# Depthwise convolutions of one layer in units of 32 channels of all batches, with the neighbouring units' preparation and finishing beside each

## Chip, cores and metric

The kernel runs on one core of a Trainium2 chip. The metric is the device time of one execution in microseconds (us); the median of several executions is given. A profile is one such execution with every engine's instructions recorded: TensorE (PE for matmuls, PEld for loading its weights), VectorE (DVE), ScalarE (ACT), GpSimd (POOL), SyncE (SP), and the DMA queues.

## The reference

Four layers, each adding a function of its group-normalised input to x of shape (4, 384, 64, 64), float32. The change is in the third, "layer 2":

```python
def layer2(x, ...):          # x: group-normalised, 4 x 384 x 64 x 64
    ...                      # gate (B), kw (B x 2, softmax): two small nets on the channel means of x
    y3 = _bn(_dw(x, c3_w, 1), c3_g, c3_b)      # depthwise 3x3
    y5 = _bn(_dw(x, c5_w, 2), c5_g, c5_b)      # depthwise 5x5
    y1 = x * c1_w + c1_b
    tok = _bn(kw[:, 0:1] * y3 + kw[:, 1:2] * y5 + y1, ar_g, ar_b)
    gp = tok.mean(axis=(2, 3), keepdims=True)
    gh = _gelu(_bn(_pw(gp, cg_w1), cg_g1, cg_b1))
    gates = sigmoid(_bn(_pw(gh, cg_w2), cg_g2, cg_b2))
    tok = tok * gates
    h1 = _gelu(_bn(_pw(tok, cm_w1), cm_g1, cm_b1))   # 384 -> 768 channels
    h2 = _bn(_pw(h1, cm_w2), cm_g2, cm_b2)           # 768 -> 384
    return gate * (tok + h2) + (1.0 - gate) * x

def _bn(x, g, b):            # statistics over batch, height and width, per channel
    m = x.mean(axis=(0, 2, 3)); v = x.var(axis=(0, 2, 3))
    return (x - m) * rsqrt(v + EPS) * g + b
```

So a channel's y3 and y5 can be normalised only when the convolution of that channel is finished in all four batches, and the gates need the mean of tok over every channel.

## The kernel before

The channels are 3 chunks (j) of 128; P = 128, N = 4096 (one image), B = 4, C = 384. Layer 2's convolutions are done on PE as products with banded matrices: the strips `z` hold, for one channel, two image rows (128 values) as partitions and (row pair, batch) as columns; `toep` is a matrix made from the channel's weights and a band of ones. One step makes both convolutions of two channels:

```python
def conv53(self, j, c0, st):                 # 64 times in a chunk
    if c0 % 8 == 0:
        self.w53 = ...                       # weights of 8 channels, DMA by SP
        self.d_o = self.bt_p.tile([P, 2, 8, P], F32, tag="d_o", name="d_o")
    t = self.bt_p.tile([P, 24, 8, 8], F32, tag="toep", name="toep53", bufs=3)
    eng, band = (nc.gpsimd, self.band7) if c0 // 2 % 5 in (1, 3) else (nc.vector, self.band7_p)
    eng.tensor_tensor(t, <w53, broadcast>, <band, broadcast>, ALU.mult)         # L1026
    m = self.psum.tile([P, 512], F32, tag="c", name="conv_m", bufs=3)
    for c in range(2):
        for i in range(3):
            nc.tensor.matmul(m[:, c * 256 : (c + 1) * 256], lhsT=self.z_[...], rhs=t[...], ...)   # L1036
    nc.scalar.copy(self.d_o[:, :, at : at + 2], mv)                              # L1045
    for c in range(2):
        for v in range(2):
            nc.vector.bn_stats(st[:, v, c0 + c], self.d_o[:, v, at + c])         # L1048
    if at == 6:
        for v in range(2):                   # 128-value runs to DRAM, on ACT's queue
            nc.scalar.dma_start(self.d53[v][j][c0 - 6 : c0 + 2].rearrange("c y b n -> (y b) c n"), self.d_o[:, v])
```

`strips5` brings x1 (the layer's input) from DRAM into strips, 1024 or 2048 values of 128 channels of one batch at a time; `to_strips5(j, b)` does so for one batch:

```python
def strips5(self, j, b, x, k0, psum):
    nc.sync.dma_start(x, self.x1[b][:, j, k0 * P : (k0 + n) * P])
    nc.scalar.activation(x, x, AF.Identity, bias=self.n2[:, j, b : b + 1], scale=self.r2[:, j, b : b + 1])
    for i in range(n // 4):
        m = psum("strip_m")
        for k in range(4):
            nc.tensor.transpose(m[:, k * P : (k + 1) * P], x[:, at : at + P], self.ident)   # L1008
        zv = self.z[:, :, 1 + k0 + 4 * i : 5 + k0 + 4 * i, b]
        if i % 2: nc.vector.tensor_copy(zv, mv)      # L1012
        else:     nc.scalar.copy(zv, mv)             # L1014
```

`conv_norms(j, st)` makes the batch norms' statistics of a chunk (two matmuls for the mean over partitions, `cn_rep`; eight into `cn_m`; a chain of small DVE operations; a root by ACT as exp and ln, L301 and L302). `toks(j)` finishes a chunk: 16 blocks, each reading x1 and the two convolutions' results from DRAM:

```python
def toks(self, j):                           # a generator; each yield ends one block
    for b in range(B):
        for q in range(4):
            src = {k: self.bc_p.tile([P, 1024], F32, tag=k, name=f"c_{k}") for k in ("x1", "d5", "d3")}
            ...                              # three DMAs by SP, L1114 and L1116
            tok = src["x1"] if j < NJ - 1 else self.tok_last[:, b, sl]
            for i in range(2):
                nc.scalar.activation(m, src["x1"][:, part], AF.Identity, bias=at(self.s0), scale=at(self.s1))     # L1123
                nc.vector.scalar_tensor_tensor(m, src["d3"][:, part], at(self.s3), m, ALU.mult, ALU.add)          # L1124
                nc.vector.scalar_tensor_tensor(tok[:, part], src["d5"][:, part], at(self.s5), m, ..., accum_out=total[...])   # L1126
            nc.scalar.activation(src["d3"], tok, AF.Square, bias=at(self.about), accum_out=squares[...])          # L1135
            if j < NJ - 1:
                nc.sync.dma_start(self.scratch["tok"][b][j][:, sl], tok)
            ...
```

`tok_last` lies in the memory of the strips, which are no longer needed then. The order of all this:

```python
def phase_b(self):
    self.to_strips5(0, B - 1)                # chunk 0's other batches were made during layer 1
    self.nets(cp)                            # the two small nets
    for j in range(NJ):
        st = ...
        toks = self.toks(j - 1)
        for c0 in range(0, P, 2):
            self.conv53(j, c0, st)
            if c0 % 10 == 8:
                next(toks, None)
        self.conv_norms(j, st)
        if j + 1 < NJ:
            for b in range(B):
                self.to_strips5(j + 1, b)
                next(toks, None)
        ...
    for _ in self.toks(NJ - 1):
        pass
```

Then `phase_ef`: the gates (a chain of small matmuls, L1196 to L1207), and the two projections. For each batch and block of 1024, the first projection:

```python
t01 = io.tile([P, NJ - 1, 1024], F32, tag="tok", name="e_tok")        # two buffers
t = [t01[:, 0], t01[:, 1], self.tok_last[:, b, blk]]
for j in range(NJ):
    if j < NJ - 1:
        nc.sync.dma_start(t[j], self.scratch["tok"][b][j][:, blk])
    nc.vector.tensor_scalar(t[j], t[j], self.at[...], self.ct[...], ALU.mult, ALU.add)   # L1235
...
for o in range(6):
    ...                                       # six matmuls 128x512 into h_s, L1250
```

## Time and profile before

Three executions: 5185.74, 5191.8 and 5192.47 us; median 5191.8. The profiled one has a span of 5184.7 us.

| engine | busy us | share | instructions |
|---|---|---|---|
| PE, matmuls | 4661.8 | 90% | 17899 |
| PEld, weight loads | 2572.5 | 50% | 17899 |
| DVE | 2773.1 | 53% | 4900 |
| ACT | 2054.1 | 40% | 2656 |
| POOL | 672.5 | 13% | 506 |

The granted clock of PE was 0.942 of full speed on average; DMA moved 723.23 MB, 139 GB/s over the span. Layer 2's convolutions begin at 2621.6 us of the span and end at 3231; the first projection's matmuls begin at 3341. In a row of groups the columns are: line, engine, operation, output and inputs, shapes, count; busy us in total and mean ns of one; then the idle time of the engine just ahead of these instructions and what ended it ("<-"). PE's records overlap in the pipeline, so the pace of a stretch of them, and not one record's length, tells what one costs.

### The profile page before, as it was taken

The page shows a single profiled execution, that of the slowest core. Times are in us where ns is not written, and L with a number is a line of the kernel's source. Part 1 is how long each engine was busy: PE and PEld are TensorE (multiplying, and loading weights), DVE is VectorE, ACT ScalarE, POOL GpSimd, SP SyncE. Part 2 cuts the span into 40 slices and gives each one's busy share as a digit, 9 for nine tenths or more (in the row PEclk, how much of TensorE's full clock was granted, in tenths as well). Part 3 has the DMA queues.
Part 4 walks back from the last instruction along what each step waited for, and adds up shares of the span by engine and source line. Part 5 has one row for each costly group of instructions (what it writes and reads, how often), then busy time and mean ns, then how long its engine had stood idle before and what let it go on. Part 6 is the DMA issues. An engine that isn't in the chain of part 4 may idle for free. (4 is left out here: it accounts for less than half of the span.)

```text
span 5184.7 us, 47837 instructions
## 1 busy us (share of the span) xinstructions
PE 4661.8 (90%) x17899; PEld 2572.5 (50%) x17899; DVE 2773.1 (53%) x4900; ACT 2054.1 (40%) x2656; POOL 672.5 (13%) x506
## 2 busy tenths in 40 slices
PE   5999999999999999999898989299999995649999
PEld 2333444334343443445377878144444442548999
DVE  5322456634565355556766988654421114658775
ACT  4544344454454444433134453511223334552320
POOL 1000000000000000000043434000000000125433
PEclk9999999999999999989988999599999997559999
DMA  5210211111111111123156989866644434557776
GB/s 163 67 48 28 88 61 61 55 62 37 60 63 66 42 43 55 61 75 100 57 169 179 348 249 284 281 227 238 246 170 166 149 134 174 215 178 247 223 222 191
DMA packets 470822, 723.23 MB, mean 139 GB/s; under 512 B 18251, under 2 KB 315958, under 8 KB 464438
## 3 DMA queue, kind: packets, MB, share of 16 engines
q1 hardware_dynamic: 330792, 519.45, 31.4%
q10 hardware_dynamic: 114510, 105.99, 6.0%
q0 software_dynamic: 25280, 94.65, 4.7%
q8 instruction: 144, 2.36, 0.2%
q14 instruction: 96, 0.79, 0.0%
HBM read 440.82 MB, written 279.18 MB: 139 GB/s over the span
## 5 line engine op out<-in xcount | busy, mean ns | idle before, releaser
L724 PE MATMUL av<-probs,vt 128*97 128x512 f32 x2048 | 955.4, 601 | 0.0
L693 ACT ACTIVATE probs<-sc_s 128x1024 f32<-128x1024 f32 x512 | 499.5, 1021 | 756.6 <-PE av L724 739.3
L724 PEld LDWEIGHTS av<-probs,vt 128*97 128x97 f32 x2048 | 319.3, 165 | 503.3 <-issue 499.7
L1036 PE MATMUL conv_m<-toep,z 128*128 128x256 f32 x2304 | 506.5, 382 | 13.0 <-ACT d_o L1045 7.6
L909 DVE SCALAR_TENSOR_TENSOR acc<-band,vecs,acc 128x512 f32<-128x512 f32 x696 | 493.5, 747 | 42.7 <-POOL band L870 25.0
L1299 PE MATMUL h_m<-f_h,cm_w_t 128*128 128x512 f32 x1152 | 496.4, 594 | 7.9 <-ACT f_h L1289 7.9
L1036 PEld LDWEIGHTS conv_m<-toep,z 128*128 128x128 f32 x2304 | 439.7, 192 | 78.5 <-issue 10.4
L1250 PE MATMUL h_s<-e_tok,cm_w_t 128*128 128x512 f32 x768 | 363.7, 596 | 5.1 <-DVE e_tok L1235 5.1
L1583 PE MATMUL conv_m<-toep,z 128*128 128x128 f32 x3072 | 363.8, 277 | 1.0 <-DVE rest_o L1591 1.0
L1299 PEld LDWEIGHTS h_m<-f_h,cm_w_t 128*128 128x128 f32 x1152 | 219.4, 191 | 284.9 <-issue 273.1
L1583 PEld LDWEIGHTS conv_m<-toep,z 128*128 128x128 f32 x3072 | 354.8, 193 | 1.5 <-issue 1.2
L1026 POOL TENSOR_TENSOR toep<-w,band 128x1536 f32<-128x1536 f32 x78 | 268.3, 3439 | 360.5 <-PE conv_m L1036 280.8
L685 PE MATMUL sc_s<-q,k 32*128 32x512 f32 x2048 | 299.6, 643 | 16.3 <-ACT probs L693 11.6
L832 PE MATMUL t_m<-w_in_t,xb 128*128 128x384 f32 x768 | 282.5, 501 | 7.9 <-DVE coef L849 3.6
L757 PE MATMUL proj_m<-xm,w_proj_t 128*128 128x512 f32 x576 | 265.2, 599 | 0.8 <-DVE xm L710 0.8
L1257 ACT COPY e_h<-h_s 128x1024 f32<-128x1024 f32 x96 | 97.2, 1012 | 398.9 <-PE h_s L1250 398.9
L764 DVE SCALAR_TENSOR_TENSOR x_res<-proj_m,bn_c,x_res 128x512 f32<-128x512 f32 x96 | 71.8, 748 | 334.2 <-PE proj_m L757 334.1
L1250 PEld LDWEIGHTS h_s<-e_tok,cm_w_t 128*128 128x128 f32 x768 | 146.9, 191 | 190.0 <-issue 184.4
L1307 DVE BATCH_NORM_STATS2 h_st<-f_h 128x6 f32<-128x512 f32 x72 | 50.0, 694 | 322.9 <-ACT f_h L1306 322.9
L1026 DVE TENSOR_TENSOR toep<-w,band_p 128x1536 f32<-128x1536 f32 x114 | 199.2, 1748 | 36.2 <-PE conv_m L1036 29.0
L832 PEld LDWEIGHTS t_m<-w_in_t,xb 128*128 128x128 f32 x768 | 141.6, 192 | 150.6 <-issue 65.5
L1045 ACT COPY d_o<-conv_m 128x512 f32<-128x512 f32 x192 | 111.1, 583 | 259.5 <-PE conv_m L1036 225.7
(360 smaller groups left out, 6328.9 us busy)
## 6 DMA issues: line engine op xcount, KB each, us to landing
d<-d_o ACTq DMA_DIRECT2D x96, 512.0 KB
c_d<-d SPq DMA_DIRECT2D x96, 512.0 KB
hid<-e_h ACTq DMA_DIRECT2D x16, 3072.0 KB
f_h<-hid SPq DMA_DIRECT2D x16, 3072.0 KB
x_res<-in_x SPq DMA_DIRECT2D x32, 768.0 KB
x_in<-in_x SPq DMA_DIRECT2D x96, 256.0 KB
xa<-x_res POOLq DMA_DIRECT2D x32, 768.0 KB, 3.9
xa_in<-xa SPq DMA_DIRECT2D x32, 768.0 KB
```

Source lines behind the costliest of these rows:

```text
L685: nc.tensor.matmul(s[:, g], lhsT=k4[32 * g : 32 * g + 32, c], rhs=q[i][32 * g : 32 * g + 32], start=True, stop=True,)
L693: nc.scalar.activation(p[:, h * 1024 : (h + 1) * 1024], s[:, 2 * h : 2 * h + 2].rearrange("p a b -> p (a b)"), AF.Exp, scale=0.25,)
L724: nc.tensor.matmul(av[0 : PD + 1, :], lhsT=vt[:, 4 * c + v, :], rhs=p[:, v * 512 : (v + 1) * 512], start=c == 0 and v == 0, stop=c == 7 an ...
L757: nc.tensor.matmul(m, lhsT=self.w_proj[:, j, o * P : (o + 1) * P], rhs=xm[:, j], start=j == 0, stop=j == NJ - 1,)
L832: nc.tensor.matmul(m[:, 0:C], lhsT=xb[:, j], rhs=self.w_in[:, j, :], start=j == 0, stop=j == NJ - 1,)
L909: nc.vector.scalar_tensor_tensor(out, src(j, k), w, done, ALU.mult, ALU.add)
L1026: eng.tensor_tensor(t, self.w53[:, at : at + 192].rearrange("p (m n) -> p m n", n=8).unsqueeze(2).to_broadcast([P, 24, 8, 8]), band.rearra ...
L1036: nc.tensor.matmul(m[:, c * 256 : (c + 1) * 256], lhsT=self.z_[:, at : at + P], rhs=t[:, 12 * c + 4 * i : 12 * c + 4 * i + 4].rearrange("p ...
L1045: nc.scalar.copy(self.d_o[:, :, at : at + 2], mv)
L1250: nc.tensor.matmul(s[:, v, :], lhsT=w1[:, j, o * P : (o + 1) * P], rhs=t[j][:, v * 512 : (v + 1) * 512], start=j == 0, stop=j == NJ - 1,)
L1299: nc.tensor.matmul(m, lhsT=w2[:, o, j * P : (j + 1) * P], rhs=h[:, o, v * 512 : (v + 1) * 512], start=o == 0, stop=o == 5,)
L1583: nc.tensor.matmul(m[:, ch * P : (ch + 1) * P], lhsT=self.z_[:, at : at + P], rhs=t[:, 8 * c + 2 * i : 8 * c + 2 * i + 2].rearrange("p m a ...
```

## The change

The convolutions are no longer done in three chunks of 128 channels with standing borders, but in 12 units of 32 channels, each of all four batches at once, so that a tile's 128 partitions are 4 batches × 32 channels. While unit u is convolved, the strips of unit u + 1 are made (odd steps) and unit u − 1 is finished (even steps). Further:

- the banded matrices are made two steps ahead, by DVE and POOL in turn (before 3 to 2);
- the statistics of two channels are taken by one instruction: it keeps those of its even and odd elements apart, and so gets the two channels' elements in turn (2 of 256 elements a step instead of 4 of 128);
- a unit's normalised x stays in SBUF for its tok; x1 is not read a second time, but chunk 0's x1 is read again, as its strips were made in another layout;
- the results of the convolutions lie in DRAM so that writes are runs of 1024 values and reads runs of 128;
- tok of every unit goes to DRAM, the last chunk's too;
- `swap` changes statistics between "a channel per partition" and "batch × 32 channels per partition", with one matmul, at the start and at the end of the stage.

```diff
 def phase_b(self):
-    self.to_strips5(0, B - 1)
+    self.taps53(0)
+    for n in range(2):
+        self.matrices53(n)
+    for q in range(4):
+        x = self.bx_p.tile([P, 2048], F32, tag="x", name="in_x1")[:, 0:1024]
+        self.strips5(0, B - 1, x, 8 * q, self.pm)
+    self.units(cp)                       # norms of x1 in the units' layout (swap)
     self.nets(cp)
-    for j in range(NJ):
-        ...
+    for _ in self.unit_strips(0):
+        pass
+    for u in range(UNITS):
+        st = self.bt_p.tile([P, 2, 16, 6], F32, tag="st", name="st")
+        strips = self.unit_strips(u + 1) if u + 1 < UNITS else iter(())
+        tok = self.unit_tok(u - 1) if u else iter(())
+        for n in range(16):
+            self.matrices53(16 * u + n + 2)
+            self.conv53(u, n, st)
+            next(strips if n % 2 else tok, None)
+        self.conv_norms(u, st)
+    for _ in self.unit_tok(UNITS - 1):
+        pass
+    self.tok_stats()                     # means and variances of tok, back by swap
...
+def unit_strips(self, u):
+    j, q = u // 4, u % 4
+    for i in range(2):
+        x = self.bx_p.tile([P, 2048], F32, tag="x", name="unit_x")      # five buffers
+        for b in range(B):
+            nc.sync.dma_start(x[32 * b : 32 * b + 32], self.x1[b][32 * q : 32 * q + 32, j, i * 2048 : (i + 1) * 2048])
+        self.unit_x[u].append(x)
+        for h in range(4):
+            if h % 2 == 0:
+                nc.scalar.activation(xh, xh, AF.Identity, bias=..., scale=...)
+            if j:
+                m = self.pm("strip_m")
+                for k in range(4):
+                    nc.tensor.transpose(m[:, k * P : (k + 1) * P], x[:, at : at + P], self.ident)
+                if h == 3:
+                    nc.vector.tensor_copy(zv.rearrange("p c k b -> p k b c"), mv)
+                else:
+                    nc.scalar.copy(zv, mv.rearrange("p k b c -> p c k b"))
+            yield
...
 # in conv53
-    for c in range(2):
-        for v in range(2):
-            nc.vector.bn_stats(st[:, v, c0 + c], self.d_o[:, v, at + c])
+    for v in range(2):
+        nc.vector.bn_stats(st[:, v, n], self.d_o[:, v, at : at + 2].rearrange("p c n -> p n c"))
...
-                self.d53[v][j][c0 - 6 : c0 + 2].rearrange("c y b n -> (y b) c n"), self.d_o[:, v]
+                self.d53[v][u][:, :, 2 * n - 6 : 2 * n + 2].rearrange("y b c n -> (y b) (c n)"),
+                self.d_o[:, v].rearrange("p c n -> p (c n)"),
...
+def unit_tok(self, u):                   # as toks, but x from self.unit_x[u], four blocks, and always:
+        nc.sync.dma_start(self.tok[u, :, :, sl].rearrange("b c n -> (b c) n"), d5)
...
 # in phase_ef
-    t = [t01[:, 0], t01[:, 1], self.tok_last[:, b, blk]]
+    at = i % 3 * 1024                    # i: the block of the batch, 0 to 3
+    t = [t01[:, 0], t01[:, 1], self.z_[:, at : at + 1024]]
     for j in range(NJ):
-        if j < NJ - 1:
-            nc.sync.dma_start(t[j], self.scratch["tok"][b][j][:, blk])
+        for q in range(4):
+            nc.sync.dma_start(t[j][32 * q : 32 * q + 32], self.tok[4 * j + q, b, :, blk])
```

`conv_norms` keeps its form, with one `cn_rep` matmul of 64 columns and four one-column matmuls into `cn_m`, once per unit.

## The prediction

> **What bounds the kernel now.** I read the page's time slices first, then windows cut at the events of layer 2, then the groups, waits and pieces of the timeline there. TensorE is busy 90% of the span, so a change here can win only where PE stands or does other work than convolving and projecting. The windows of layer 2's convolutions and what follows (columns: length; busy us and instructions of PE, weight load, DVE, ACT, POOL; granted clock; DMA share; GB/s):
>
> ```profile
> 2621.60:2792.00 170.40, 169.75 (x774) 147.93 (x774) 121.67 (x310) 52.38 (x83) 88.98 (x26) 0.99 0.50 142
> 2792.00:2840.00 48.00, 32.42 (x149) 24.80 (x149) 28.38 (x52) 31.90 (x35) 0.33 (x1) 0.68 0.77 225
> 2840.00:3019.00 179.00, 170.44 (x768) 146.94 (x768) 160.07 (x400) 79.70 (x125) 89.28 (x26) 0.98 0.93 304
> 3019.00:3059.00 40.00, 26.40 (x139) 19.04 (x139) 24.33 (x45) 28.64 (x31) 0.18 (x1) 0.83 0.86 251
> 3059.00:3231.00 172.00, 168.51 (x780) 146.32 (x778) 160.03 (x405) 74.45 (x124) 86.06 (x25) 1.00 0.92 292
> ```
> ```profile
> 3231.00:3325.00 94.00, 5.45 (x20) 4.42 (x20) 54.30 (x144) 46.53 (x72) 0.00 (x0) 0.52 1.10 326
> 3325.00:3341.00 16.00, 1.90 (x12) 1.73 (x12) 9.20 (x38) 13.78 (x20) 0.00 (x0) 0.50 0.28 110
> 3341.00:3840.00 499.00, 497.14 (x1151) 219.80 (x1152) 252.11 (x386) 99.73 (x101) 11.50 (x16) 0.99 0.60 225
> ```
>
> Lines 1, 3 and 5 are the three chunks of convolutions, PE all but full. Lines 2 and 4 are the borders: statistics, then the strips of the next chunk (transposes and copies), with no convolution. The first line of the second fence is the tail: the last chunk's tok, PE empty, DMA over its full share. Then the small chain of gates, then the projections, PE full again. In 2621.6–3341 PE convolves in five sixths of the time; the rest is what the change aims at. The waits of 3231–3345 say what each engine of the tail stands for:
>
> ```profile
> PE cg_z L1201 <- DVE gp L1196: 90.2, 1, 90.2
> DVE tok_m L1124 <- DMA c_d<-d: 20.4, 12, 3.1
> ```
>
> PE has one wait of 90.2 us, for channel means that need all of tok; inside it DVE waits for tiles from DRAM. A block of tok (1024 of a batch) starts every 4.9 us there. The price list of the operations concerned, from the groups of 2540–3300:
>
> ```profile
> L1026 POOL TENSOR_TENSOR toep<-w,band 128x1536 f32<-128x1536 f32 x78 | 268.3, 3439 | 360.5 <-PE conv_m L1036 280.8 <-DVE toep L1026 35.1 <-DMA w<-in_c_t 19.4
> L1026 DVE TENSOR_TENSOR toep<-w,band_p 128x1536 f32<-128x1536 f32 x114 | 199.2, 1748 | 36.2 <-PE conv_m L1036 29.0 <-issue 6.9
> L1048 DVE BATCH_NORM_STATS2 st<-d_o 128x6 f32<-128x128 f32 x768 | 165.5, 280 | 35.1 <-ACT d_o L1045 35.0
> L1045 ACT COPY d_o<-conv_m 128x512 f32<-128x512 f32 x192 | 111.1, 583 | 259.5 <-PE conv_m L1036 225.7 <-DMA d<-d_o 30.5 <-issue 2.1
> L1014 ACT COPY z<-strip_m 128x512 f32<-128x512 f32 x36 | 38.4, 1072 | 28.4 <-PE strip_m L1008 28.4
> L1012 DVE COPY z<-strip_m 128x512 f32<-128x512 f32 x36 | 38.7, 1074 | 29.2 <-PE strip_m L1008 29.1
> ```
>
> The borders are seen to the microsecond in the timeline: convolution resumes at these points (start, length; in brackets the wait ahead):
>
> ```profile
> 2839.97 23.55 PE L1036 MATMUL conv_m<-toep,z 128*128 128x256 f32 x108 [1.26 <-DVE z L1012]
> ...
> 3341.03 6.55 PE L1250 MATMUL h_s<-e_tok,cm_w_t 128*128 128x512 f32 x8 [5.08 <-DVE e_tok L1235]
> ```
>
> [...] 0.52 in the tail against 0.99 to 1.00 beside it, so every long stand costs a little more after it. [...] the trace shows 1.28 us. Twelve statistics chains instead of three bring more loads. [...] chunk 1, mostly 512-byte pieces, moves 142 GB/s at a share of 0.50 (284 per full share), the projections, in larger pieces, 225 at 0.60 (375). So the 4-KB writes of the new layout should help. [...] DVE's toep reads its band from PSUM, and of POOL's idle time only 35.1 us are put down to DVE's toep. I count POOL at its 3.44 us.
>
> **The change part by part.**
>
> *Convolutions themselves.* In the undisturbed 2700–2750 PE does 233 records in 50.00 us, 0.2146 each; a step of two channels has 12, so 2.575 us; 192 steps are 494.4 us. This stays. Before, 2621.6–3231 is 609.4: 494.4, borders of 48.6 (2791.4 to 2839.97) and 44.1 (3018.3 to 3062.46), and 22.3 lost inside the chunks.
>
> *Borders.* What goes is their standing. The transposes do not: chunks 1 and 2 need 64 groups of four at 0.66 us (one such group in the timeline), 42.2 us of PE between convolutions. So of 92.7 us at most 50.5 come free.
>
> *New on PE's path.* Statistics run 12 times, each with a rep matmul, four small ones, and some waiting for DVE between: I estimate 1.8 us of PE each, 22, mostly because PE's queue runs in order and holds the next convolution back. The last transposes of a unit stand right ahead of the next unit's first convolution in PE's order, whose copy by ACT or DVE (1.07) and semaphores cost an estimated 2 us at the eight such borders: 16. Inside losses 10 to 15 instead of 22.3, since the stats and writes are lighter but tok and strips run beside every step. The first steps of the stage: 4.
> Sum: 494.4 + 42.2 + 22 + 16 + 4 + 12 = 590.6, against 609.4: −19.
>
> *Other engines, per unit of 16 steps (about 49 us).* DVE: 8 toep × 1.75 = 14.0; statistics 32 of 256 elements, from 0.22 at 128 and 0.64 at 512 in runs, about 0.36 each, 11.5 (before 64 × 0.22 = 14); two strip copies 2.1; tok 8 × (0.75 + 0.74 + 0.08) = 12.6; the chain 3.3. Together 43.5, 89%. ACT: d_o 16 × 0.58 = 9.3, normalise and tok about 4.2 + 6.2, Squares 5.4, six strip copies at 0.64 to 1.07, table loads and DMA issues: some 39. POOL: 8 × 3.44 = 27.5. None exceeds PE, but DVE runs in order with little room. DMA: 2.1 MB of x, 1.6 of taps, 4.2 written, 4.2 read, 2.1 of tok: 14.2 MB in 49 us, 290 GB/s; chunk 2 ran at 304. It fits, with no reserve.
>
> *Start.* The first strips come in quarters with copies behind them, against whole halves: −4, an estimate; the new layout exchange (one small matmul) eats little of it.
>
> *Tail.* From the last convolution (3231) to the first projection (3341.03) are 110 us, 94 of them for a whole chunk's tok. Now one unit, a twelfth, is left: statistics 11 (before, first tok at 3247.6, but with larger statistics and weight loads ahead of it), writing and reading the last convolutions (inside that and a few us more), four blocks at an estimated 3.2 (4.9 × 2 of 3 tiles read), 27 to here; final sums and layout exchange 4; the gates' chain 16, plus some 3 as its weights' DMAs are issued by ACT only behind the last Square. Together 50: −60.
>
> *Projections.* All tok comes from DRAM now, four DMAs of 32 partitions per chunk. Chunk 2's third uses three places in the strips' buffer, by block number modulo 3; block 3 of a batch and block 0 of the next share place 0, so that load waits for the last matmul of the block. The block's last group leaves PE 4 matmuls × 0.854 = 3.4 us of other work; load, scale and start I put at 8 (estimate from the 4.9 us cadence with DVE behind it). +4.5 at three borders: +13.
>
> Sum: −4 −19 −60 +13 = −70; 5191.8 − 70 = 5122.
>
> **The rivals.** (a) *The convolution stage gains nothing or grows.* In its favour: chunk 2's DVE was at 160.07 of 179 us with the load now spread over all units; DVE waits in order for tok's reads, and a late read holds up toep, hence PE; twelve statistics chains with ACT's table loads. Against: the matrices are two steps ahead and the stats are cheaper. It would turn the −19 into 0 to +40: 5141 to 5181. (b) *All of it hides.* If transposes fill PE's gaps without stops, statistics cost 1 us, and the projections never wait, the floor is 494.4 + 42.2 + 12 + 10 = 559, tail 45, no projection loss: −50 −65 −4 = −119, about 5073. Against: two dozen handovers between engines in each unit. (c) *The projections turn DMA-bound.* They read 8.4 MB more than before in the same 499 us, 17 GB/s over 225 at a share of 0.60: as a rate no danger; only the shared place speaks for it. If each of 16 blocks waited 3 us, +48: 5160.
>
> **Range and chances.** The tail is the sure part (−50 to −65). The convolution stage runs from −45 to +20 about −19, the projections 0 to +30. Together 5085 to 5168 in eight of ten. Two per cent is 5088: faster 0.13, within 0.84, slower (over 5295.6) 0.03.
>
> **What would show it.** Right: first convolution to last about 590 us, PE's clock near 1.0 with no window of it under 0.9; the gap from the last convolution to the first h_s about 50, clock at half in it; in the projections three waits of h_s for DVE's scaling of the strips' buffer, about 4.5 each; toep 96 on each engine, statistics 384 of 256. Wrong: statistics nearer 0.55 each than 0.36 (reading every second channel may be slow), which would put 6 us more on DVE per unit and make it the bound; POOL's toep well above 3.44; long conv_m waits for toep; or the tail at 70 because of late weights.

## The result and the profile after

Four executions of the changed kernel: median 5163.4 us (5156.27 to 5167.02), against 5192.1 for the kernel before (four executions, 5185.74 to 5192.96). The ratio is 0.9946, with a 95% interval of 0.9928 to 0.9963. The kernel is faster by 28.7 us, half a per cent; the prediction was 5122, a gain of 70.

The two profiled executions, cut at the same events of PE (first and last convolution of layer 2, first product of the first projection, first of the second):

| stretch | before, us | after, us | change | predicted |
|---|---|---|---|---|
| start of the span to layer 1's last norm | 2599.6 | 2607.4 | +7.8 | 0 |
| from there to the first convolution | 22.0 | 21.0 | −1.0 | −4 |
| convolutions, first to last | 609.3 | 627.7 | **+18.4** | **−19** |
| tail: last convolution to first h_s | 110.1 | 54.8 | −55.2 | −60 |
| projections: first h_s to first h_m | 507.5 | 524.4 | +16.9 | +13 |
| the rest | 1336.2 | 1330.0 | −6.2 | 0 |

The first and last rows are work that the change does not touch; over all runs of this study the first lies between 2599 and 2613. So totals below are compared by medians of several executions, and stretches by profiles. The tail and the projections came out within 5 us of what was predicted. The convolutions (from here on "the stage") were to give 19 us and took 18 more.

Windows of the changed kernel (columns as in the prediction's windows; units 0 to 3, units 4 to 10, unit 11, the tail, the projections):

```profile
2628.40:2849.00 220.60, 191.20 (x843) 163.58 (x839) 164.56 (x316) 109.45 (x164) 110.03 (x32) 0.93 0.75 225
2849.00:3210.10 361.10, 330.78 (x1638) 286.00 (x1638) 295.18 (x603) 207.75 (x322) 192.83 (x56) 1.00 0.92 275
3210.10:3256.20 46.10, 44.53 (x200) 38.40 (x200) 38.48 (x85) 22.87 (x37) 20.67 (x6) 0.96 0.88 274
3256.20:3311.00 54.80, 4.16 (x25) 3.52 (x25) 23.80 (x95) 28.34 (x41) 0.00 (x0) 0.55 0.89 258
3311.00:3827.50 516.50, 503.83 (x1152) 221.81 (x1152) 258.35 (x391) 99.67 (x101) 11.47 (x16) 0.98 0.63 233
```

No engine is full in the first line: of 220.6 us DVE works 164.56, ACT 109.45, POOL 110.03. PE's 191.20 contains time at a granted clock of 0.50 (30.7 of the 220.6 us; 0.93 on average). Units 4 to 10 take 361.10 / 7 = 51.6 us each, every one alike; the prediction's 590.6 is 49.2 on average. Units 0 to 3 take 55.3, 53.7, 50.7 and 60.9, although units 0 to 2 have no transposes beside them, as chunk 0's strips were made during layer 1. Of the names below, `d_o` is ACT's copy of a convolution's result out of PSUM, `unit_x` a unit's x, `st` a unit's statistics, `cn_...` and `about` the values of the chain that `conv_norms` makes of them ("the chain"), `c_d` and `tok_m` tok in the making.

What PE waited for between the first and last convolution (columns: us in total, times, longest):

```profile
PE conv_m L1122 <- ACT d_o L1131: 17.6, 9, 5.6
PE strip_m L1051 <- ACT unit_x L1044: 11.7, 8, 1.8
PE cn_rep L1149 <- DVE st L1134: 7.2, 9, 1.5
PE conv_m L1122 <- DVE toep L1103: 5.5, 3, 3.2
PE conv_m L1122 <- DVE about L1189: 5.4, 1, 5.4
```

PE waits for ACT to empty a PSUM buffer, once in each of nine units (first line), and eight times for x that ACT has yet to normalise (second). The last line bears the name of the last DVE operation that ended before PE went on, but no convolution reads `about`. The timeline of unit 3 (columns: start, length, engine, instruction; in brackets the wait ahead) shows what PE waited for:

```profile
2802.65 3.41 POOL L1103 TENSOR_TENSOR toep<-w,band 128x1536 f32<-128x1536 f32 x1 [1.75 <-PE conv_m L1122]
2802.86 3.22 DVE L1186 TENSOR_TENSOR about<-c_u,cn_s 128x1 f32<-128x1 f32 x1
...
2806.00 1.74 DVE L1103 TENSOR_TENSOR toep<-w,band_p 128x1536 f32<-128x1536 f32 x1
...
2807.89 1.19 PE L1122 MATMUL conv_m<-toep,z 128*128 128x256 f32 x2 [5.39 <-DVE about L1189]
```

DVE's matrix for this step ended at 2807.74, 0.15 us ahead of PE, and stood behind an addition of one column that took 3.22 us. Another 1.3 us, at the start of unit 3, are put down to `cn_d` in the same way. So matrices (toep), which the prediction watched, cost PE 5.5 + 5.4 + 1.3 = 12.2 us, all of them DVE's; no wait of PE is put down to one of POOL's. The groups of the same operations in the changed kernel:

```profile
L1103 POOL TENSOR_TENSOR toep<-w,band 128x1536 f32<-128x1536 f32 x96 | 330.4, 3442 | 313.3 <-PE conv_m L1122 254.3 <-issue 35.3 <-DMA w<-in_c_t 14.5
L1103 DVE TENSOR_TENSOR toep<-w,band_p 128x1536 f32<-128x1536 f32 x96 | 166.1, 1745 | 11.0 <-PE conv_m L1122 10.8
L1134 DVE BATCH_NORM_STATS2 st<-d_o 128x6 f32<-128x256 f32 x384 | 149.7, 423 | 87.4 <-ACT d_o L1131 87.0
L1189 DVE TENSOR_TENSOR about<-about,cn_mean 128x1 f32<-128x1 f32 x24 | 28.4, 1183 | 0.1
```

POOL's and DVE's matrices have the durations that were taken for them (3442 and 1745 ns). The statistics take 423 ns each; by the prediction's measure, busy time over count, they take 0.39 us (149.7 / 384), not 0.36. The last line is the odd one: 24 additions of one column take 1183 ns on average. Seen one by one (columns: shortest, median, longest ns, first and last start) they are mostly short:

```profile
L1189 DVE TENSOR_TENSOR about<-about,cn_mean x24: 136/160/3354, 2704.1 to 3263.5; 128x1 f32<-128x1 f32 x24
```

Ten of over 2 us make up 26 of the 28.4.

Unit 5, one of the seven alike, shows what happens:

```profile
2912.25 3.45 POOL L1103 TENSOR_TENSOR toep<-w,band 128x1536 f32<-128x1536 f32 x1 [2.21 <-PE conv_m L1122]
...
2913.14 2.58 DVE L1189 TENSOR_TENSOR about<-about,cn_mean 128x1 f32<-128x1 f32 x1
...
2915.64 0.74 DVE L1212 SCALAR_TENSOR_TENSOR tok_m<-c_d,cn_s,tok_m 128x512 f32<-128x512 f32 x1
2916.30 0.15 DVE L1189 TENSOR_TENSOR about<-about,cn_mean 128x1 f32<-128x1 f32 x1
...
2918.76 0.73 DVE L1214 SCALAR_TENSOR_TENSOR c_d<-c_d,cn_s,tok_m 128x512 f32<-128x512 f32 x1
...
2919.53 1.15 ACT L1219 ACTIVATE c_d<-c_d,about 128x1024 f32<-128x1024 f32 x1 [5.64 <-DVE c_d L1214]
...
2920.68 0.56 ACT L1131 COPY d_o<-conv_m 128x512 f32<-128x512 f32 x1
...
2921.38 1.53 PE L1122 MATMUL conv_m<-toep,z 128*128 128x256 f32 x6 [1.51 <-ACT d_o L1131]
```

POOL's matrix runs from 2912.25 to 2915.70. DVE's addition starts inside it and ends at 2915.72. Its twin, a moment later and outside POOL's matrix, takes 0.15. The 2.4 us go down the chain: DVE's tok is late, ACT's Square (L1219) stands 5.64 for it, the next d_o copy is behind the Square in ACT's order and starts at 2920.68, though its convolutions ended at 2914.70, and PE, whose three PSUM buffers are full, stands 1.51. It was not the matrix that came late: that of this step, POOL's of 2912.25, had been ready for 5.7 us. Then PE stands 1.4 more for a transpose, as ACT comes late to normalise x as well. In unit 1 the same chain made PE stand 5.6 and then work for 3.0 us at a granted clock of 0.50 (2712.49 to 2715.52).

The whole stage shows the same: of DVE's additions, products and differences with both inputs in SBUF that began while at least 0.5 us of one of POOL's matrices was left (2400 to 3300 us), 16 of 16 lasted to that matrix's end. Of tok's operations of 128x512 with one input in PSUM, 77 did so and none was held (at most 0.775 us). What in the chip makes it so, no run shows.

The tail and the projections of the changed kernel, PE's longest waits:

```profile
PE swap_m L1021 <- DVE swap L1019: 26.1, 1, 26.1
PE cg_z L1292 <- DMA cg_w_t<-in_cg_w_t: 13.4, 1, 13.4
```
```profile
PE h_s L1342 <- DVE z L1327: 12.6, 4, 4.0
PE h_s L1342 <- DVE e_tok L1327: 5.1, 1, 5.1
```

PE first stands 26.1 us for the last unit's tok, then 13.4 for the gates' weights. In the projections it stands four times, 12.6 us together, for chunk 2's scaling in the strips' buffer: 1.6 in the first block (1.8 before), and 3.9, 4.0 and 3.2 at the three borders between batches. The 5.1 is the start, 5.08 before.

### The profile page after: what moved, and what is told of

Its sections match the earlier page's. It is cut to its first block, busy times and chain, and to the rows that moved or that the text cites. A ratio compares the mean times of both kernels' runs of the same rounds, so it can differ in the third digit from the quotient of the medians.

```text
span 5165.3 us, 48069 instructions
## 1 busy us (share of the span) xinstructions
PE 4669.4 (90%) x17963; PEld 2579.1 (50%) x17963; DVE 2742.2 (53%) x4606; ACT 2093.9 (41%) x2736; POOL 734.3 (14%) x524
## 5 line engine op out<-in xcount | busy, mean ns | idle before, releaser
L1122 PE MATMUL conv_m<-toep,z 128*128 128x256 f32 x2304 | 527.4, 389 | 33.5 <-ACT d_o L1131 17.6
L1103 POOL TENSOR_TENSOR toep<-w,band 128x1536 f32<-128x1536 f32 x96 | 330.4, 3442 | 313.3 <-PE conv_m L1122 254.3
L1351 DVE BATCH_NORM_STATS2 h_st<-e_h 128x6 f32<-128x512 f32 x192 | 123.4, 685 | 203.7 <-ACT e_h L1349 203.7
L1342 PE MATMUL h_s<-z,cm_w_t 128*128 128x512 f32 x384 | 198.3, 600 | 12.6 <-DVE z L1327 12.6
```

The source lines that it names most:

```text
L1103: eng.tensor_tensor(t, self.w53[:, at : at + 192].rearrange("p (m n) -> p m n", n=8).unsqueeze(2).to_broadcast([P, 24, 8, 8]), band.rearra ...
L1342: nc.tensor.matmul(s[:, v, :], lhsT=w1[:, j, o * P : (o + 1) * P], rhs=t[j][:, v * 512 : (v + 1) * 512], start=j == 0, stop=j == NJ - 1,)
L1351: nc.vector.bn_stats(st[:, o, 8 * b + 2 * i + v, :], h[:, o, v * 512 : (v + 1) * 512])
```

## The experiments

Theory A: the small operations of the statistics chain are held by POOL's matrices, and that delay goes through ACT's order to PE. Theory B: the chain, with ACT's table loads and twelve handovers, is long by itself, or ACT and DVE are simply too full; the long additions are only where the waiting shows. Further questions were what the chain costs in all, the place shared in the projections, late weights at the start and in the tail, and what the two other parts of the change (two channels in one instruction, longer runs) are worth. All ratios are to the kernel before on the same chip; its medians there lay between 5187.9 and 5194.2 us, so medians of different runs are compared to within some 6 us only.

| run | median us | ratio, 95% interval | convolutions, us |
|---|---|---|---|
| after | 5163.4 | 0.9946 (0.9928 to 0.9963) | 627.7 |
| e1: chain with one input in PSUM | 5183.4 | 0.9977 (0.9967 to 0.9987) | 645.5 |
| e2: no chain in units 1 to 11 | 5117.3 | 0.9855 (0.9832 to 0.9878) | 586.8 |
| e3: own place per block | 5148.5 | 0.9919 (0.9896 to 0.9941) | 625.4 |
| e4: taps earlier | 5160.1 | 0.9938 (0.9915 to 0.9961) | 623.8 |
| e5: no matrices by POOL | 5107.5 | 0.9842 (0.9816 to 0.9867) | 568.4 |
| e6: short chain | 5120.2 | 0.9856 (0.9827 to 0.9886) | 581.6 |
| e7: short chain, Sqrt | 5124.8 | 0.9877 (0.9851 to 0.9904) | 575.1 |
| e8: gates' weights early | 5166.1 | 0.9949 (0.9929 to 0.9968) | 625.0 |
| e9: together | 5102.7 | 0.9811 (0.9787 to 0.9835) | 576.4 |
| e10: e6, four statistics a step | 5128.9 | 0.9880 (0.9863 to 0.9897) | 596.9 |
| e11: matrices 3 to 2 | 5144.1 | 0.9899 (0.9881 to 0.9917) | 607.0 |
| e12: e6, runs of 512 bytes | 5125.2 | 0.9866 (0.9851 to 0.9882) | 588.5 |

### e1: the chain with one input in PSUM

```diff
-        mean = self.sm([P, 2], "cn_mean")
+        mean = own(64, 2)          # own: 80 columns of the PSUM bank that holds DVE's band
-            nc.vector.tensor_mul(a[:, v : v + 1], a[:, v : v + 1], ...)
+            nc.vector.tensor_mul(a_s[:, v : v + 1], a[:, v : v + 1], ...)     # a in PSUM, a_s in SBUF
...                                 # and so on: of two inputs always one in PSUM
```

> In the changed kernel the twelve statistics chains hold DVE operations of one or two columns that last up to 3.35 us instead of 0.15, always until a banded matrix on POOL ends. Here each such operation reads one of its two inputs from PSUM, and the copy of the means into four blocks is an addition of a zero from PSUM; the values are the same. Theory A (DVE is locked out by POOL while it reads two SBUF inputs, ACT stands behind the chain with the copies that free the convolution's PSUM, and so PE stands): no operation of the chain over 0.7 us, the stalls of 5 to 6 us of PE in the first four units gone, convolution stage 627.8 to about 605, time about 20 us below the changed kernel. Rival B (the lock is on DVE's slack; PE stands because ACT runs in order behind tok's squares anyway): the operations are short, but the stage stays within 6 us of 627.8.

Nothing is left out. All long operations are gone: DVE's time above each operation's own shortest falls from 63 to 21 us in the stage, and none is over by more than 0.3. Yet the stage is longer, 645.5. The scratch lay in the tile of DVE's band, and so the whole chain was put ahead of DVE's next toep, which came late. PE's wait for it in unit 5 (2906.1 to 2961.4) of this run, one of ten in the stage with 37.8 us together:

```profile
PE conv_m L1126 <- DVE toep L1107: 4.5, 1, 4.5
```

So both expectations of the time missed. The run shows that a PSUM input frees these operations of the hold; on its worth for the time it says nothing, since it put another wait in place of the first.

### e2: no statistics chain

```diff
-                self.conv_norms(u, st)
+                if u == 0:
+                    self.conv_norms(u, st)
```

> Leaves out the statistics chain of 11 of the 12 units (scale and shift of the first unit are used for all), so no rep and four-block matmuls, no table loads and no small DVE operations in them; everything else stays. Upper bound of what the chains cost. Theory A: stage 627.8 to about 590 (1.6 us of PE's own work and 2 us or more of waiting in each of 11 units). Rival B: stage stays above 612, only PE's own 1.6 us a unit goes.

This leaves out the batch norms' chain of units 1 to 11; they use unit 0's scale. The stage falls by 40.9 us, 3.7 for each chain left out. PE's own `cn_rep` and `cn_m` are 20.9 in all, 1.7 a unit. So about 2 us a unit is what the chain does to others, and this run alone cannot say whether by its length (B) or by being held (A).

### e3: a place of its own for each block in the projections

```diff
-                    at = i % 3 * 1024
+                    at = i * 1024
```

> The third chunk's tok takes four places in the strips' buffer (block number), not three, so a block never shares its place with the one just before it. If the shared place makes the projections' loss (h_s waits 12.6 us for DVE's scaling of that buffer, 4 times): those waits of 3 to 4 us at the batch borders go, projections 524.4 to about 513, time about 11 us below the changed kernel, the convolution stage unchanged. Rival (loads of tok are late for other reasons, such as more and smaller DMAs in SP's queue): the waits stay at about 12 us and the time the same.

The projections fall from 524.4 to 507.0, before's 507.5, and the convolutions hardly move (627.7 to 625.4). The waits of the same stretch in this run:

```profile
PE h_s L1342 <- DVE z L1327: 1.2, 1, 1.2
PE h_s L1342 <- DVE e_tok L1327: 5.1, 1, 5.1
```

The whole loss in the projections was the shared place; the 8.4 MB that are read in addition show no cost, as the prediction had it.

### e4: weights of the convolutions loaded earlier

```diff
             self.taps53(0)
+            self.taps53(4)
...
-            self.taps53(n + 4)
+            self.taps53(n + 8)     # three buffers instead of two
```

> Weights of the banded matrices are loaded eight steps ahead instead of four (three buffers instead of two), so the third load stands in SP's queue before the loads of the next unit's x, which at the start wait for a semaphore that ACT's first result DMA releases at 2653 us. If that queue makes the first unit's stall: POOL's 14.5 us wait for the weights and PE's 3.2 us wait for a matrix go, first unit 55.3 to about 49, time some 5 us below the changed kernel. Rival (the stall only moves to the next thing that is late in unit 0): first unit within 2 us of 55.

POOL had stood 14.5 us for weights in unit 0. That wait is gone, but unit 0 is no shorter (56.6 against 55.3). In unit 0 of this run:

```profile
POOL toep L1105 <- issue: 33.7, 4, 14.1
...
PE conv_m L1124 <- DVE toep L1105: 3.2, 1, 3.2
```

POOL now stands as long for nothing that the profile names ("issue"), and PE's 3.2 for DVE's toep are unchanged: POOL's lateness was not on the path. Units 1 and 3 became 43.9 and 64.5 (53.7 and 60.9 in the changed kernel). These units have the same work as before; what moved is when POOL's matrices fall against the chain. That fits A, but this run alone does not show it.

### e5: no matrices by POOL

```diff
+        if n % 2:
+            self.toep[n] = self.toep_even      # the even step's matrix again
+            return
```

> Leaves out POOL's banded matrices: every odd step convolves with the matrices of the step before it, so POOL does nothing in the stage, and DVE and ACT have exactly what the changed kernel gives them, statistics chains included. The first test of the lock (chain operations with a PSUM input) removed every long operation but put the chain in one piece ahead of DVE's matrices, and the stage grew to 645.5. Theory A (what makes the chains dear is that POOL's matrices lock DVE out): no DVE operation of the chain over 0.7 us, units of the later chunks 51.6 to about 48.5, stage 627.8 to about 600. Rival B (chains are dear by themselves, by their length in DVE's, ACT's and PE's in-order queues with two table loads): operations short, but units stay at 50.5 or more and the stage above 615.

This leaves out the odd steps' matrices and uses the even ones twice; every second channel pair is convolved with the weights of the pair before it. PE, ACT and DVE have the same work as in the changed kernel; only POOL is empty. The windows (whole stage, and unit 5) and three groups of this run:

```profile
2621.40:3189.80 568.40, 552.04 (x2681) 480.52 (x2677) 454.85 (x1000) 340.84 (x522) 0.00 (x0) 0.99 0.94 284
2856.20:2904.40 48.20, 46.82 (x234) 40.90 (x234) 40.05 (x87) 29.84 (x46) 0.00 (x0) 1.00 0.96 294
```
```profile
L1192 DVE TENSOR_TENSOR about<-about,cn_mean 128x1 f32<-128x1 f32 x24 | 3.8, 157 | 0.7
L1160 DVE COPY cn_four<-st 128x256 f32<-128x256 f32 x12 | 3.9, 324 | 0.1
L311 ACT ACT_TABLE_LOAD x17 | 21.8, 1283 | 5.4 <-DMA e_tok<-tok 4.3 <-ACT d_o L1134 0.9
```

The 24 additions take 157 ns, not 1183. The stage falls by 59.3 us, units 1 and 2 to 43, units 4 to 10 to 48.2 (one 49.9). The chain is there in full, with its table loads. So B falls: the chain, ACT and DVE as they are allow 568, and POOL's matrices beside them cost 59. (POOL's waits for weights are gone too; e4 took those alone away, for 4.) The stage is also 18.4 shorter than in e2, which has one chain but all of POOL's matrices: 23 shorter in units 0 to 3 (209.9 in e2, 186.5 here), 5 longer in the others. In unit 0, which has no chain yet, an operation of the small nets on three numbers takes over 3 us beside POOL (3.16 in the changed kernel), and PE waits 4.0 for what follows it, here 0.7; in unit 1 e2 still has unit 0's chain with three long operations. In units 2 and 3 of e2 PE stands 2.4 and 3.2 for DVE's matrices; why is not shown.

### e6: a short chain

```diff
+    # once: gk = gamma * k, base = c1_b + sum of beta * k, about = -c1_u - base
-        ...                        # 15 DVE operations on one or two columns, and the root
+        self.rsqrt(m[:, 6:8], m[:, 2:4])                        # in PSUM
+        nc.vector.tensor_mul(s, m[:, 6:8], self.gk[:, u])
+        nc.vector.scalar_tensor_tensor(c, m[:, 0:2], -1.0, s, ALU.mult, ALU.mult, accum_out=c0)
+        nc.scalar.activation(s0, c0, AF.Identity, bias=self.base[:, at])
```

> Same results from a shorter chain: what does not hang on the statistics (weights times batch-norm factors, the offset, the mean of tok) is made once for all units, so a unit's chain has 3 DVE operations and one on ACT behind the two of the root, instead of 16, none of the 3 with two SBUF inputs. Theory A (locks): the 25 us of long additions and nearly all other excess go; stage about 605, time 20 us below the changed kernel. Rival B (length of the queue with its two table loads): half of it, stage about 615. If it is below 600, both the lock and the length count.

Nothing is left out: in `about` the statistics cancel (minus the mean times the scale in the shift, plus the same in the mean of tok), so it is made once for all units. Of 15 DVE operations behind the small matmuls, two remain, with one PSUM input each. POOL works as in the changed kernel (323 us in the stage), and the work is otherwise the same. Unit 5 of this run, as window and timeline:

```profile
2882.10:2930.30 48.20, 46.80 (x234) 40.97 (x234) 38.50 (x75) 30.02 (x47) 27.53 (x8) 1.00 0.96 295
```
```profile
2891.33 9.01 PE L1137 MATMUL conv_m<-toep,z 128*128 128x256 f32 x41
...
2893.65 0.75 DVE L1213 SCALAR_TENSOR_TENSOR tok_m<-c_d,cn_s,tok_m 128x512 f32<-128x512 f32 x1
2893.80 3.44 POOL L1118 TENSOR_TENSOR toep<-w,band 128x1536 f32<-128x1536 f32 x1 [2.21 <-PE conv_m L1137]
...
2897.41 1.15 ACT L1220 ACTIVATE c_d<-c_d,about 128x1024 f32<-128x1024 f32 x1 [2.49 <-DVE c_d L1215]
```

With POOL at work the unit takes 48.2, as without POOL in e5. POOL's matrix meets DVE's tok, and tok, with an input in PSUM, runs on beside it; the Square waits 2.49 instead of 5.64 and PE is not stopped. The stage is 581.6; the 13 us above e5 lie in units 0 to 3. There copies of `cn_four` from SBUF to SBUF are still held (0.32 us, up to 2.31), and once the operation ahead of one, `cn_d<-st,cn_d` with both inputs in SBUF (3.11); PE waits for `cn_four` 1.9 to 2.1 us in each of units 1 to 3. This is the repair of the failed term: 46 us of the stage and 43 of the median. It changes two things, the form of the operations and their number; that the number alone is not what costs is shown by e5, which has the long chain.

### e7: the short chain with another root

```diff
-        self.rsqrt(m[:, 6:8], m[:, 2:4])                        # exp and ln, two table loads
+        nc.scalar.activation(m[:, 6:8], m[:, 2:4], AF.Sqrt, bias=self.eps)
+        nc.vector.reciprocal(m[:, 6:8], m[:, 6:8])
```

> As the short chain, with the root as ACT's square root and a reciprocal on DVE, in place of logarithm and exponential, which take a table load of 1.28 us each in every unit. If table loads stand on the chain's path (rival B): 11 x 2.5 us of ACT less, stage another 5 to 12 us below the short chain's. If the lock alone counts (theory A): within 3 us of it.

One of the table-load groups of this run, and then the same line of e6:

```profile
L311 ACT ACT_TABLE_LOAD x6 | 7.7, 1283 | 4.5 <-DMA e_tok<-tok 4.4
```
```profile
L311 ACT ACT_TABLE_LOAD x18 | 23.1, 1283 | 7.3 <-DMA e_tok<-tok 4.4 <-ACT d_o L1146 2.7
```

The steady units are 48.2 in both, so table loads, which rival (a) named, are not on PE's path there. The stage is 6.5 shorter, which as a number lies in B's 5 to 12; but it comes from units 0, 3 and 10 alone, not from every unit, and the medians (5124.8 and 5120.2) do not show it. A share of the loads in those three units is not excluded.

### e8: the gates' weights loaded early

```diff
+            self.cg1 = self.z_[:, 16904:16976]...       # unused columns of the strips' buffer
+            self.cg2 = self.z_[0:24, 16980:17364]
+            nc.scalar.dma_start(...)                    # both, ahead of the two small nets
```

> The two small weights of the gates are loaded at the start of the stage into unused columns of the strips' buffer, not behind the last square of tok, where ACT's queue issues them and PE then waits 13.4 us for their landing (10 of it behind the normalisation's own chain). If the weights set the end of the tail: gap from the last convolution to the first projection 54.8 to about 48, time 6 us below the changed kernel. Rival (the tok loads of the projections or the normalisation's chain end last): the gap stays within 2 us.

The 13.4 us wait is gone and the tail is 45.4 instead of 54.8. What remains ahead of the gates is this:

```profile
PE cg_z L1295 <- DVE gp L1290: 5.2, 1, 5.2
```

But the median is 5166.1, not below the changed kernel's 5163.4. In the profile the stretch ahead of the first convolution is 25.1 us and the projections 527.7, 4 and 3 more (2 of the 3 in the first block's wait for chunk 2, 3.6 instead of 1.6); but e3 and e7, without these loads, have 25.2 ahead of the first convolution too. So the wait was taken away, and a gain in the whole time is not shown.

### e11: matrices 3 to 2 again

```diff
-        eng, band = (nc.gpsimd, self.band7) if n % 2 else (nc.vector, self.band7_p)
+        eng, band = (nc.gpsimd, self.band7) if n % 5 in (1, 3) else (nc.vector, self.band7_p)
```

> The changed kernel with the matrices shared 3 to 2 between DVE and POOL as in the kernel before, not 1 to 1; nothing else. Theory A (POOL's matrices lock DVE's chain out): POOL is busy 22 instead of 27.5 us a unit, so fewer and shorter locks; stage 627.8 to about 615 although DVE has 2.8 us a unit more. Rival (DVE's load bounds the stage): units 51.6 to 53 or more, stage above 640.

The split of the kernel before, with the long chain. The stage is 607.0, 20.7 less than after, though DVE, the fuller engine, has more to do: it makes a fifth more of the matrices. Units 4 to 10 vary from 49.4 to 52.6, as POOL's matrices fall at other points of each. Were DVE too full, as B has it, the stage would have grown. But A's "fewer and shorter locks" is not what the trace shows: operations over their shortest by more than 0.3 us are 14 against 17, and are held for 36 us together against 39. What changed is which operations are held, and when. So the new 1:1 split of the matrices, one of the small parts of the change, cost some 20 us by itself, through the places of the meetings rather than their number; how a place turns into PE's time was followed in units 3 and 5 of the changed kernel only.

### e10 and e12: two other parts of the change, undone in e6

```diff
-        for v in range(2):
-            nc.vector.bn_stats(st[:, v, n], self.d_o[:, v, at : at + 2].rearrange("p c n -> p n c"))
+        for c in range(2):
+            for v in range(2):
+                nc.vector.bn_stats(st[:, v, 2 * n + c], self.d_o[:, v, at + c])
```

> The short chain (5120 us) with the statistics as before: four of 128 elements a step, not two of 256, so each channel has two halves and the chain works on twice the columns with twice the small matmuls. If one instruction for two channels is worth much (DVE as the bound): DVE 2 us a unit more, units 48.2 to 50 or more, time +20. Rival (768 x 0.22 against 384 x 0.39 is nearly the same busy time, and DVE has room): units within 1.2 us of 48.2, what they grow by being PE's own second matmuls, time +5 to +15.

The statistics of this run, 768 of 128 elements as before the change:

```profile
L1152 DVE BATCH_NORM_STATS2 st<-d_o 128x6 f32<-128x128 f32 x768 | 172.9, 281 | 80.3 <-ACT d_o L1148 80.2
```

They take 172.9 us of DVE against 149.7 for 384 of 256, only 1.9 us a unit. Steady units are 49.3 (two of seven 51.0) instead of 48.2; 0.8 of the 1.1 are PE's additional small matmuls, as the even and odd halves have to be joined. Taking two channels in one instruction is worth about 1.1 us a unit, less through DVE than through PE.

```diff
-            [self.dram.tile([32, B, 32, P], ...)
+            [self.dram.tile([32, B, 32, 144], ...)[:, :, :, 0:P]      # rows padded: writes in runs of 128 values
```

> The short chain (5120 us) with rows of the convolutions' results padded in DRAM, so that writes are runs of 512 bytes as before, not 4 KB; same bytes, reads and order. If the long runs are what lets 14 MB pass in a unit: DMA share 0.9 to above 1.0 in the later units, units 48.2 to 50 or more, time +20 or more. Rival (DMA has room at 275 GB/s): share up to 1.0 at most, units within 0.5 us of 48.2, time within 5 us.

Most of units 5 to 8 of this run (2877.8 to 3075.4), and units 4 to 10 of e6:

```profile
2882.10:3075.00 192.90, 184.37 (x919) 160.09 (x918) 150.76 (x287) 118.15 (x187) 108.57 (x32) 1.00 1.05 289
```
```profile
2833.90:3173.40 339.50, 329.50 (x1638) 287.87 (x1638) 269.21 (x519) 210.04 (x329) 192.71 (x56) 0.99 0.96 292
```

At 512 bytes a run the 16 DMA engines are busy 1.05 of the window for 289 GB/s (275 per full share), with 4-KB runs 0.96 for 292 (304). Units 4 to 10 take 49.4 on average with short runs, 48.5 in e6. So the longer runs are worth about 1 us a unit, between what the two theories had.

### e9: what is worth keeping, together

```diff
+        # e6's short chain, e3's place, e8's weights, and:
-        eng, band = (nc.gpsimd, self.band7) if n % 2 else (nc.vector, self.band7_p)
+        eng, band = (nc.gpsimd, self.band7) if n % 2 and n >= 12 else (nc.vector, self.band7_p)
```

> All that helped, together: the short chain, four places for the third chunk's tok, the gates' weights loaded early; and the first twelve steps' matrices all on DVE, as the nets of the first unit also stand behind POOL's matrices (3.16 us for an operation of three numbers). If the parts add: stage 581.6 less some 6 in the first unit, tail about 45, projections about 507; time 5163 - 43 - 15 - 9 - 6, about 5090, the floor rival of the prediction nearly reached (its 2% limit 5088). If the parts cover one another: above 5105.

Median 5102.7 (5082.91 to 5110.35), 0.9811 of the kernel before and 61 us under the changed one: faster than both. It is 13 above the sum of the parts, and below the 5105 of parts that cover one another. Convolutions, tail and projections of this run:

```profile
2630.90:3207.20 576.30, 554.54 (x2679) 483.37 (x2676) 456.34 (x881) 342.61 (x534) 309.94 (x90) 0.99 0.92 280
3207.20:3253.70 46.50, 4.39 (x26) 3.68 (x25) 21.55 (x83) 28.59 (x42) 0.00 (x0) 0.54 0.88 270
3253.70:3766.10 512.40, 499.88 (x1153) 220.60 (x1153) 261.80 (x398) 106.33 (x109) 11.47 (x16) 0.98 0.66 242
```

The first twelve steps' matrices on DVE alone shortened unit 0 from 54.0 (e6) to 49.6. The projections kept a wait of 4.6 us for DVE's scaling, in their first block and not at a border, so they gave 12.0 of e3's 17.4.

## Why the prediction was wrong, point by point

**Convolutions themselves: right.** 192 steps at 2.575 us are 494.4; e5, with nothing held, spends 511.6 at convolutions, and the steady units of e6 41.7 each against 494.4 / 12 = 41.2. (One reading beside it is wrong: of 2621.6–3341 PE convolves not five sixths but 521.4 of 719.4 us, 72%, by the prediction's own windows; five sixths is the stage with its borders. No sum rests on it.)

**Transposes and statistics on PE: right.** 42.2 and 22 were predicted, 40.0 and 20.9 measured.

**Handovers, first steps and inside losses: the step that failed.** The prediction put them at 16 + 4 + 12 = 32 us and said "inside losses 10 to 15 instead of 22.3, since the stats and writes are lighter". PE spent 565.4 us at convolutions, so 71 were lost, 39 more than allowed; that is the whole miss of the stage (627.7 against 590.6) but for 2 us of the two terms above. The wait that it left out is that of small DVE operations for POOL's matrices. This is shown: taking the matrices away, with the whole chain in place, brings 59.3 us (e5), and a short chain with PSUM inputs 46 with the matrices in place (e6). In units 4 to 11 both take away the same, 25 us. Of the 71, 40 lie in units 0 to 3 (205.2 us at convolutions, 4 × 41.2 at full pace), where PE twice stood over 5 us and had 31 of the stage's 34 us at a granted clock of 0.50; there e6 brings 21 and e5 34. For the 13 between them the runs show copies of `cn_four` and an operation of the nets held, but not that these make up all of it.

Without the hold, the sum would have erred the other way: 568.4 in e5, 581.6 in e6, against 590.6. Rival (b)'s floor of 559 was near. The idea of the change was sound; a part that seemed not to belong to it took the gain back. Of the signs of being wrong that the prediction named, one came in part: waits for DVE's matrices, 12.2 us, of which 5.4 behind a held addition of the chain.

**What was read too narrowly.** Of what DVE and POOL do to each other the prediction looked at one operation (DVE's toep, with its band in PSUM: 1.755 us at most in 23 meetings with POOL's matrices, 1.745 on average over all) and at POOL's side (3.44 us, and 3442 ns was measured). POOL's matrices stay at 3.41 to 3.46 us; the small operations of DVE are the ones that grow. And the chain was priced by its sum, 3.3 us a unit, from chains that ran at the borders with POOL empty (0.33 and 0.18 us of POOL in the two border windows that the prediction shows). The change put eleven of its twelve among POOL's matrices. The trace of the kernel before had the sign already, in an operation off PE's path, at the end of a chunk's tok beside the convolutions of the next:

```profile
L1146 DVE TENSOR_TENSOR tok_off<-mvt,about x12: 155/164/3004, 2855.8 to 3323.7; 128x1 f32<-128x1 f32 x12
```

The shortest is 155 ns and the longest 3004 for the same shape. Five of the twelve began inside one of POOL's matrices and lasted to its end. Nothing waited for them, so no list of waits showed them, and a mean over a group hides them.

**Rival (a)** had the sign and the size (0 to +40; +18.4 measured). Of its reasons, DVE's fixed order with toep behind late work is part of the mechanism (in unit 3 PE stood 5.39 us for a matrix behind an addition of 3.22), the twelve chains too; table loads are not in the steady units (e7). That POOL's matrices would make the work late, it did not say.

**Other engines.** DVE 42.2 us a unit (43.5 predicted), POOL 27.5 (27.5), ACT 29.7 (39 predicted, but with DMA issues, which the profile does not count as busy). As predicted none exceeds PE; it did not help, since the loss came from order, not from load.

**Start:** −1 instead of −4. **Tail:** 54.8 instead of 50. To the end of tok 27 were predicted, and PE's wait for it is 26.1; the gates' weights cost PE 13.4 where 3 was allowed for, of which 9.4 go with early loads (e8). **Projections:** +16.9 instead of +13, by the cause named: three waits of 4.5 at the borders were predicted, and three of 3.9, 4.0 and 3.2 came; e3 takes the whole loss away. (That estimate counts four matmuls at 0.854 us as PE's other work. In the changed kernel 34 of them took 14.59 us from 3424.56 on, 0.43 each; with that, 6.3 would have followed.)

**Sum:** −70 predicted, −28.7 by the medians. By the profiles the stage is 37 us off, the other three terms together 12. The time lies inside the range given, near its upper end.

## What to carry to other kernels

When work that stood alone is moved beside a GpSimd stream, list every DVE operation that comes to lie there, the smallest too, look at its longest duration and not its mean, and ask where its inputs are: with both in SBUF an addition of one column took up to 3.35 us here, beside GpSimd instructions of 3.44, and the order of DVE's and ACT's work handed that on to PE (5.39 us in unit 3, 1.51 in unit 5). Take out of such a chain what does not depend on the late data, and give what is left one PSUM input (in e1 none was then over its shortest by more than 0.3 us), but not in a tile that the path needs (e1 again: ten waits of PE, 37.8 us); and when splitting work between DVE and GpSimd, count what GpSimd's share does to the rest of DVE (59.3 us of the stage, e5).

## What the runs showed of the hardware

- In the changed kernel 16 of 16 additions, products and differences of one column by DVE, with both inputs in SBUF, that began with at least 0.5 us left of a GpSimd multiplication of 128x1536, its inputs in SBUF too, lasted to that one's end: 0.15 us became up to 3.35 (3.40 in e11; 64 columns 3.11 once in e6), while GpSimd's own stayed at 3.41 to 3.46. With one input in PSUM none was held: 128x512 took at most 0.775 us in 77 meetings, 128x1536 1.755 in 23. Two products of two columns in e11 (0.15 us) were not held though both inputs lay in SBUF: they began 11 and 13 ns after GpSimd's multiplication, the twelve that were held over 1 us to its end in that run 46 ns or more.
- A copy of 128x256 from SBUF to SBUF is held too (0.32 us, up to 2.31); so was an operation with one SBUF input and a number on 128x4 (`gx`, 3.41 us once in the kernel before, 0.16 in the changed one); a copy of one column was not, in 10 meetings (at most 0.154 us); statistics, with one input, were not, in 156 (at most 0.455).
- Behind PE's stands of 5.59 and 5.39 us in units 1 and 3 its granted clock was 0.50 for the first 3.0 and 3.2 us of work; in the kernel before, behind the tail, for the first 5.8 (3341.03 to 3346.80). Over units 4 to 10, with four stands of 1.5 us, it was 1.00.
- One batch-norm statistics instruction over two channels taken in turn (256 elements) takes 0.42 us, two over 128 elements 0.56.
